# Cross-attention slots: the probabilities' split moved to the head of the slot, the value product into the same slot, the bias a slot behind its load

## The chip, the cores and the metric

One core of one Trainium2 chip runs the whole kernel. The metric is device time in microseconds (us). The kernel before takes 2206.15 us, the median of three runs (2199.84 to 2209.55).

## What is computed

For each of 32 batches there are 512 query rows of 640 channels (`x`) and 77 context rows of 1024 channels (`ctx`), all in float32. There are 20 heads of 32 channels.

```python
q   = heads(x @ to_q_w)
k,v = heads(ctx @ to_k_w), heads(ctx @ to_v_w)
p   = softmax(q @ k.T / sqrt(32))          # 77 keys for each head
out = merge(p @ v) @ to_out_w + to_out_b + x
```

The reference also slices further groups of context rows (object, others, ip) behind row 77. The context has only 77 rows, so these groups are empty and the kernel computes the text branch alone.

Float32 products are made from two parts: a value is split into a high part (a copy rounded to the matmul type) and a low part (value minus high part), and three of the four cross products are summed in PSUM (`PAIRS`). That is why nearly every operand is first copied on ScalarE and then subtracted on VectorE or GpSimd.

## The kernel before, in words

A first phase (lines 210 to 239, up to about 280 us) makes keys, values and split weights from the context and leaves them in DRAM (`k_dram`, `v_dram`, `wo_dram`). Then comes a loop over 160 *slots*: slot n handles batch b = n // 5 and head group j = n % 5 (four heads). All engines get their instructions in the order in which `slot` (lines 522 to 595) writes them; nothing reorders them, so an instruction that waits holds up all that stands behind it on its engine. DMAs are all issued by SyncE (SP), one queue, in the same written order.

For slot n the steps are these. Times of a step are in the profile under the line given.

- `scores(n, t)`, t = 0 to 3 (L335): three matmuls into one of three `sc` banks, then VectorE's maximum (L343). `exps(n, t)` (L353): four exponentials on ScalarE, which write probabilities into one of two buffers `pn` and row sums.
- `normalize(n-1)` (L364, L365): VectorE's reciprocal of the sums, then GpSimd multiplies the previous slot's probabilities in place.
- `transpose_p(n-1)` (L372, L379): VectorE transposes them into the single buffer `z`; four DMAs write `z` to the DRAM scratch `pd`.
- `load_p(m)` (L388, L389): two DMAs read `pd` of an older slot m back, with keys on the partitions, into the single buffer `raw`.
- `cast_p(m)` (L396, ScalarE, 128x1024) and `rest_p(m)` (L402 VectorE, L405 ScalarE 64x512, L406 GpSimd): split `raw` into `pp`, two buffers. This is "the split of probabilities". In the steady state it is done three slots after the scores, m = n-3 (`SPLIT_LAG`), between the second and third scores of slot n.
- `values(m)` (L420): eight matmuls of `pp` with the values `vb` into the one bank `pa`, then `split_a` into `at`. It is done four slots after the scores, m = n-4 (`TAKE_LAG`).
- `queries(n+1)` (L317): fifteen matmuls into the single bank `pq`, then `split_q` (L100 ScalarE, L101 VectorE) into one of two `qt`, which `scores(n+1, ...)` need.
- `piece(b', i)` (L449): the output projection of an older batch, in ten pieces of twelve matmuls, two pieces in each slot. `finish` (L477, L481): VectorE adds a finished bank to the residual row block `xr`, and SP writes it out. `load_residual` and `add_bias` (L438, L442) load `xr` (two buffers) and add the bias on GpSimd, both in the same slot.
- `load_x` (L256), `transpose_x` (L261), `split_x` (L268, L269): the next batch's `x`, single buffer `xs`, is loaded at the start of a slot with j = 4, transposed in j = 0 and 1, and split in j = 2 (two of five) and j = 3 (three of five). `queries` needs it in the slot j = 4.
- `refill` (L294, L304): keys of heads j = 0, 1 are reloaded in j = 2, those of j = 2, 3, 4 in j = 1; values of j = 0, 1 in j = 3 and those of j = 2, 3, 4 in the next batch's j = 0. A values load is seven DMAs in pieces of 77, 48, 29, 77, 16, 61 and 61 rows, and each row is cut into runs of 256 bytes.

The first four slots run beside the end of the context phase. Buffers `raw`, `pp`, `at`, `xr` and the weights `wo_s` exist only from slot 4 on (`LATE`). After slot 159, `end` (lines 597 to 643) splits and multiplies what is still under way, makes the last pieces of batch 30 and the whole projection of batch 31; its residual blocks are loaded one by one in the last loop (line 639).

Of the kernel before, what the change touches and what calls it, by code (L numbers as in the profile page):

```python
# [50 lines left out]
def kernel(  # L51
# [207 lines left out]
    def transpose_x(b, i):  # L259
        part = xss[b][:, 4 * i : 4 * i + 4, :].rearrange("p a u -> p (a u)")  # L260
        nc.vector.transpose(part, part)  # L261
# [67 lines left out]
    def scores(n, t):  # L329
        b, j = divmod(n, NC_)  # L330
        g = GROUP_OF[j]
        qt, kb = qts[n % 2], kbs[g][:, j - GROUPS[g][0]]
        sc = ps.tile([P, S], F32, tag="sc", name="sc", bufs=3)
        for m, (a, c) in enumerate(PAIRS):
            nc.tensor.matmul(  # L335
                sc[:, :KCOLS],
                qt[:, a, t * P : (t + 1) * P],
                kb[:, c, :],
                start=(m == 0),
                stop=(m == 2),  # L340
            )
        nm = main.tile([P, HPC], F32, tag="nm", name="nm", bufs=2)
        nc.vector.tensor_reduce(  # L343
            nm, sc[:, :KCOLS].rearrange("p (h k) -> p h k", k=NKEY), AX.X, ALU.max, negate=True
        )
        return sc, nm
# [11 lines left out]
                accum_out=sms[n][:, at : at + 1],  # L358
            )

    def normalize(n):
        pf = pnb[n % 2][:, :, :NKEY]
        rs = main.tile([P, NQ * HPC], F32, tag="rs", name="rs", bufs=2)
        nc.vector.reciprocal(rs, sms.pop(n))  # L364
        nc.gpsimd.tensor_tensor(  # L365
            pf, pf, rs.unsqueeze(2).to_broadcast([P, NQ * HPC, NKEY]), ALU.mult
        )
# [16 lines left out]

    def load_p(n):
        pd = pds.pop(n)
        raw = late[0].tile([P, 3, S], F32, tag="raw", name="raw", bufs=1)
        nc.sync.dma_start(raw[:, 0:2, :], pd[0 : 2 * P, :].rearrange("(k p) q -> p k q", p=P))  # L388
        nc.sync.dma_start(raw[:64, 2, :], pd[2 * P :, :])  # L389
        raws[n] = raw  # L390

    def cast_p(n):

        raw = raws[n]
        pp = late[0].tile([P, 5, S], FPR, tag="pp", name="pp", bufs=2)
        nc.scalar.copy(pp[:, 0:2, :], raw[:, 0:2, :])  # L396
        pps[n] = pp

    def rest_p(n):

        raw, pp = raws.pop(n), pps[n]
        nc.vector.tensor_tensor(  # L402
            pp[:, 2:4, :], raw[:, 0:2, :], pp[:, 0:2, :].bitcast(F32), ALU.subtract
        )
        nc.scalar.copy(pp[:64, 4, :], raw[:64, 2, :])  # L405
        nc.gpsimd.tensor_tensor(  # L406
            pp[64:, 4, :], raw[:64, 2, :], pp[:64, 4, :].bitcast(F32), ALU.subtract
        )
# [24 lines left out]
        split(at[:, 0, :], at[:, 1, :], pas.pop(n))  # L433
        ats[n] = at

    def load_residual(b, t):
        xr = late[0].tile([P, C], F32, tag="xr", name="xr", bufs=2)
        nc.sync.dma_start(xr, x[b, t * P : (t + 1) * P, :])  # L438
        xrs[b, t] = xr

    def add_bias(b, t):
        nc.gpsimd.tensor_tensor(xrs[b, t], xrs[b, t], bias, ALU.add)  # L442
# [37 lines left out]
            if h == 1:  # L480
                nc.sync.dma_start(out[b, t * P : (t + 1) * P, :], xr)  # L481

    def residual(b, t):
        load_residual(b, t)
        add_bias(b, t)

    LATE = 4
    SPLIT_LAG, TAKE_LAG = 3, 4

    splits = {LATE: [0], LATE + 1: [1, 2], LATE + 2: [3]}  # L490
    takes = {LATE + 1: [0], LATE + 2: [1, 2], LATE + 3: [3]}
    for n in range(4, N):
        splits[n + SPLIT_LAG] = [n]
        takes[n + TAKE_LAG] = [n]


    PIECES = {3: (1, 0), 4: (1, 2), 0: (2, 4), 1: (2, 6), 2: (2, 8)}
    RESIDUAL = {3: (1, 0), 4: (1, 1), 0: (2, 2), 1: (2, 3)}
    TRANSPOSE_X = {0: (0, 1), 1: (2, 3)}
    SPLIT_X = {2: ((), (0,), (1,)), 3: ((2,), (3,), (4,))}  # L500
    wos = []

    def take(m):
# [2 lines left out]

    def refill(b, j):

        if j == 0 and b >= 2:
            load_values(b - 1, 1)  # L510
        elif j == 1 and b >= 1:
            load_keys(b, 1)
        elif j == 2 and b + 1 < B:
            load_keys(b + 1, 0)
        elif j == 3 and b >= 1:
            load_values(b, 0)
        elif j == 4 and b + 2 < B:
            load_x(b + 2)
        elif j == 4 and b == B - 1:
            load_values(b, 1)  # L520

    def slot(n, beside=None):
        b, j = divmod(n, NC_)
        ahead = n + 1 < N
        back, first = PIECES[j]
        bo_, has_out = b - back, b >= back
        xsplits = SPLIT_X.get(j, ((), (), ())) if b + 1 < B else ((), (), ())
        turns = list(TRANSPOSE_X.get(j, ())) if b + 1 < B else []
        taken, split_now = takes.get(n, []), splits.get(n, [])

        has_residual = j in RESIDUAL and b >= RESIDUAL[j][0]
        upcoming = splits[n + 1][0] if late and splits.get(n + 1, [N])[0] in pds else None

        refill(b, j)
        if n:
            normalize(n - 1)
        s = scores(n, 0)
        finish()
        exps(n, 0, *s)
        if ahead:  # L540
            queries(n + 1, 0, 2)
        s = scores(n, 1)
        if has_residual:
            load_residual(b - RESIDUAL[j][0], RESIDUAL[j][1])
        if n:
            transpose_p(n - 1)
        exps(n, 1, *s)
        for m in split_now[:1]:
            cast_p(m)
        if ahead:  # L550
            queries(n + 1, 2, NC_)
        s = scores(n, 2)
        for m in split_now[:1]:
            rest_p(m)
        for m in split_now[1:]:
            load_p(m)
        if upcoming is not None and len(split_now) < 2:
            load_p(upcoming)
        if has_residual:
            add_bias(b - RESIDUAL[j][0], RESIDUAL[j][1])  # L560
        for c in xsplits[0]:
            split_x(b + 1, c)
        if ahead:
            split_q(n + 1)
        exps(n, 2, *s)
        if has_out:
            piece(bo_, first)
            if j == 2:
                piece(bo_, first + 1)
        finish()  # L570
        for i in turns[:1]:
            transpose_x(b + 1, i)
        for c in xsplits[1]:
            split_x(b + 1, c)
        for m in taken[:1]:
            values(m)
        if beside:
            beside()
        s = scores(n, 3)
        for m in taken[:1]:  # L580
            split_a(m)
        for c in xsplits[2]:
            split_x(b + 1, c)
        exps(n, 3, *s)
        for m in taken[1:]:
            take(m)
        for m in split_now[1:]:
            cast_p(m)
            rest_p(m)
        if upcoming is not None and len(split_now) > 1:  # L590
            load_p(upcoming)
        if has_out and j != 2:
            piece(bo_, first + 1)
        for i in turns[1:]:
            transpose_x(b + 1, i)

    def end():


        last = B - 1  # L600
        normalize(N - 1)
        cast_p(N - 3)
        rest_p(N - 3)
        finish()
        transpose_p(N - 1)
        load_p(N - 2)
        take(N - 4)
        residual(last - 1, 2)
        for i in (4, 5):
            piece(last - 1, i)  # L610
        cast_p(N - 2)
        rest_p(N - 2)
        load_p(N - 1)
        take(N - 3)
        finish()
        residual(last - 1, 3)
        for i in (6, 7):
            piece(last - 1, i)
        take(N - 2)
        finish()  # L620
        for i in (8, 9):
            piece(last - 1, i)
        cast_p(N - 1)
        rest_p(N - 1)
        finish()
        for i, (t, h) in enumerate((t, h) for t in range(NQ) for h in range(2)):
            if i < 3:
                pos[last, t, h] = ps.tile([P, S], F32, tag="sc", name="po", bufs=3)
            elif i == 3:
                pos[last, t, h] = ps.tile([P, S], F32, tag="pq", name="po", bufs=1)  # L630
            elif i < 7:
                output_bank(last, t, h)
            else:
                take(N - 1)
                pos[last, t, h] = late[1].tile([P, S], F32, tag="pa", name="po", bufs=1)
            for j in range(4):
                project(last, t, h, j)
        for t in range(NQ):
            residual(last, t)
            for h in range(2):  # L640
                project(last, t, h, 4)
                closed.append((last, t, h))
            finish()

    with tc.manual_schedule(engines=ENGINES):
# [23 lines left out]
            ctx.enter_context(tc.tile_pool(name="psl", bufs=1, space=PSUM, reuse_waits="tile"))  # L669
        )  # L670
        load_p(0)
        wos.append(late[0].tile([P, NC_, 2, C], FPR, name="wo_s"))
        for n in range(LATE, LATE + 4):
            slot(n)
# [45 lines left out]
```

## Time and profile before

| | |
|---|---|
| median of the three runs | 2206.15 us |
| profiled execution, its own time | 2202.92 us |
| its span | 2201.1 us |
| mean granted TensorE clock | 0.98 |
| TensorE matmul busy / weight load busy | 2042.4 us (93%) / 1802.9 us (82%) |
| ScalarE / VectorE / GpSimd busy | 1381.1 (63%) / 1234.3 (56%) / 1036.1 (47%) |
| DMA: mean share of 16 engines, rate | 72.8%, 188 GB/s |
| first scores of slot 8 on TensorE | 375.3 us |
| end of TensorE's work of slot 159 | about 2123.8 us |

The profile is of one execution, so durations taken from it add up to its own time and not to the median. PE is TensorE's matmul, PEld its weight load, DVE VectorE, ACT ScalarE, POOL GpSimd and SPq SyncE's DMA queue. Matmuls overlap in the pipeline, so a busy PE is not a PE without loss; the wait of the weight loads shows more of it than the wait of the matmuls.

### The profile page before, as it was taken

The numbers are of one execution on the slowest core, as the hardware profiler recorded it, in microseconds if no ns is written. First come the engines' busy times: TensorE is split into PE (matmuls) and PEld (weight loads), VectorE is DVE, ScalarE is ACT, GpSimd is POOL, SyncE is SP. The second block draws the span as 40 slices with busy tenths as digits, with TensorE's granted clock in tenths as the row PEclk, the third lists the DMA queues.
The fourth block names the chain that finished last, engine by engine and source line by source line (L and its number), as shares of the span: only waits on it lengthen the run. The fifth ranks groups of instructions, "written<-read, shape, count | busy, mean of one in ns | idle before, by whom it ended". The sixth has DMA issues, their size and how long they took to land.

```text
span 2201.1 us, 36626 instructions
## 1 busy us (share of the span) xinstructions
PE 2042.4 (93%) x11012; PEld 1802.9 (82%) x11012; DVE 1234.3 (56%) x1996; ACT 1381.1 (63%) x6057; POOL 1036.1 (47%) x618
## 2 busy tenths in 40 slices
PE   9899997999999999999999999999999999999985
PEld 7799975888888888888888888888888888888875
DVE  4433245566665666665566656566556566656651
ACT  3322156677677676777767777776666676777750
POOL 0000134555555555555555555555555555555542
PEclk9999998999999999999999999999999999999998
DMA  8953358877777777777877777787777777778662
GB/s 190 274 164 112 110 120 213 207 204 193 200 201 198 192 196 204 197 185 200 207 200 188 202 195 202 197 205 196 197 200 188 198 198 194 200 198 203 176 172 95
DMA packets 524243, 416.45 MB, mean 189 GB/s; under 512 B 138480, under 2 KB 427760, under 8 KB 524048
## 3 DMA queue, kind: packets, MB, share of 16 engines
q1 hardware_dynamic: 524048, 414.13, 72.8%
q8 instruction: 89, 1.46, 0.3%
q14 instruction: 106, 0.87, 0.1%
HBM read 238.69 MB, written 175.31 MB: 188 GB/s over the span
## 4 chain that ended last, share of the span: by engine, by line
DMA 31%; PE 23%; SPq 12%; issue 10%; POOL 9%; ACT 7%; DVE 6%; POOLq 0%; DVEq 0%; ACTq 0%
DMA raw<-pd 16%; DMA xr<-in_x_dram 7%; PE pk L164 5%; SPq L379 5%; PE pq L317 5%; PE po L449 5%; POOL xt L269 5%; PE pv L190 4%; DMA out_dram<-xr 4%; POOL pn L365 4%; ACT pn L353 3%; PE pa L420 2%; ACT pp L396 2%; PE sc L335 2%; SPq L304 2%
## 5 line engine op out<-in xcount | busy, mean ns | idle before, releaser
L353 ACT ACTIVATE pn<-sc,nm 128x77 f32<-128x77 f32 x2560 | 796.3, 332 | 366.2 <-DVE nm L343 362.6
L317 PE MATMUL pq<-xt,wq_s 128*128 128x512 f32 x2400 | 643.9, 404 | 29.8 <-POOL xt L269 28.2
L449 PE MATMUL po<-wo_s,at 128*128 128x320 f32 x3840 | 609.9, 309 | 9.3 <-DVE xr L477 7.9
L449 PEld LDWEIGHTS po<-wo_s,at 128*128 128x128 f32 x3840 | 573.4, 188 | 12.0 <-DVE xr L477 9.0
L317 PEld LDWEIGHTS pq<-xt,wq_s 128*128 128x128 f32 x2400 | 439.4, 192 | 139.4 <-POOL xt L269 63.2
L353 ACT ACTIVATION_READ_ACCUMULATOR pn<-sc,nm 128x1 f32 x2560 | 539.8, 211 | 0.0
L372 DVE STREAM_TRANSPOSE z<-pn 128x1280 f32<-128x1280 f32 x160 | 241.9, 1512 | 393.9 <-POOL pn L365 392.8
L335 PE MATMUL sc<-kb,qt 128*128 128x308 f32 x1920 | 392.5, 311 | 74.7 <-ACT qt L100 38.6
L335 PEld LDWEIGHTS sc<-kb,qt 128*128 128x128 f32 x1920 | 327.7, 190 | 139.3 <-ACT qt L100 49.1
L406 POOL TENSOR_TENSOR pp<-raw,pp 64x512 fp32r<-64x512 f32 x160 | 266.2, 1664 | 367.8 <-ACT pp L405 365.3
L442 POOL TENSOR_TENSOR xr<-xr,bias 128x640 f32<-128x640 f32 x128 | 201.6, 1575 | 447.4 <-DMA xr<-in_x_dram 374.2
L365 POOL TENSOR_TENSOR pn<-pn,rs 128x1232 f32<-128x1232 f32 x160 | 364.1, 2276 | 49.8 <-DVE rs L364 46.5
L420 PE MATMUL pa<-pp,vb 128*128 128x512 f32 x1280 | 329.1, 400 | 14.4 <-DVE at L101 14.4
L343 DVE TENSOR_REDUCE nm<-sc 128x4 f32<-128x308 f32 x640 | 278.7, 445 | 37.2 <-PE sc L335 36.8
L420 PEld LDWEIGHTS pa<-pp,vb 128*128 128x128 f32 x1280 | 244.8, 197 | 52.9 <-DVE at L101 15.3
L396 ACT CAST pp<-raw 128x1024 fp32r<-128x1024 f32 x160 | 169.1, 1057 | 183.0 <-DMA raw<-pd 181.5
L402 DVE TENSOR_TENSOR pp<-raw,pp 128x1024 fp32r<-128x1024 f32 x160 | 214.4, 1340 | 89.5 <-ACT pp L396 89.5
L269 POOL TENSOR_TENSOR xt<-xs,xt 128x512 fp32r<-128x512 f32 x160 | 201.9, 1284 | 30.5 <-POOL pp L406 12.9
L477 DVE TENSOR_TENSOR xr<-po,xr 128x320 f32<-128x320 f32 x256 | 117.4, 479 | 103.1 <-POOL xr L442 100.4
L164 PE MATMUL pk<-ct,wk_s 128*128 128x512 f32 (+1 forms) x600 | 137.3, 391 | 9.8 <-ACT ct L100 9.8
L190 PE MATMUL pv<-wv_s,ct 128*128 128x320 f32 (+1 forms) x960 | 142.1, 309 | 0.0
L190 PEld LDWEIGHTS pv<-wv_s,ct 128*128 128x128 f32 (+1 forms) x960 | 139.4, 184 | 2.0
(36 smaller groups left out, 1075.1 us busy)
## 6 DMA issues: line engine op xcount, KB each, us to landing
pd<-z SPq DMA_DIRECT2D x640, 160.0 KB
raw<-pd SPq DMA_DIRECT2D x160, 512.0 KB
xs<-in_x_dram SPq DMA_DIRECT2D x128, 320.0 KB
xr<-in_x_dram SPq DMA_DIRECT2D x128, 320.0 KB
out_dram<-xr SPq DMA_DIRECT2D x128, 320.0 KB
raw<-pd SPq DMA_DIRECT2D x160, 128.0 KB
v_dram<-vs SPq DMA_DIRECT2D x19, 640.0 KB
k_dram<-ks SPq DMA_DIRECT2D x20, 512.0 KB
```

The costliest lines, as they stand in the source:

```text
L164: nc.tensor.matmul(pks[j][:, :gn], wk_s[:, k, a, j * P : (j + 1) * P], cts[k][:, c, :gn], start=(k == 0 and n == 0), stop=(k == NK - 1 and ...
L190: nc.tensor.matmul(pv[:tn, :HALF], cts[k][:, a, t0 : t0 + tn], wv_s[:, k, c, h * HALF : (h + 1) * HALF], start=(k == 0 and n == 0), stop=( ...
L269: nc.gpsimd.tensor_tensor(parts[1], src, parts[0].bitcast(F32), ALU.subtract)
L317: nc.tensor.matmul(pqs[n], wq_s[:, k, a, j * P : (j + 1) * P], xts[b, k][:, c, :], start=(k == 0 and m == 0), stop=(k == NC_ - 1 and m == 2),)
L335: nc.tensor.matmul(sc[:, :KCOLS], qt[:, a, t * P : (t + 1) * P], kb[:, c, :], start=(m == 0), stop=(m == 2),)
L343: nc.vector.tensor_reduce(nm, sc[:, :KCOLS].rearrange("p (h k) -> p h k", k=NKEY), AX.X, ALU.max, negate=True)
L353: nc.scalar.activation(pnb[n % 2][:, at, :NKEY], sc[:, i * NKEY : (i + 1) * NKEY], AF.Exp, bias=nm[:, i : i + 1], accum_out=sms[n][:, at : ...
L365: nc.gpsimd.tensor_tensor(pf, pf, rs.unsqueeze(2).to_broadcast([P, NQ * HPC, NKEY]), ALU.mult)
L372: nc.vector.transpose(z.rearrange("p b t j -> p t b j"), pn.rearrange("p (t h) k -> p t (h k)", t=NQ).rearrange("p t (b i) -> p t b i", i=Q),)
L406: nc.gpsimd.tensor_tensor(pp[64:, 4, :], raw[:64, 2, :], pp[:64, 4, :].bitcast(F32), ALU.subtract)
L420: nc.tensor.matmul(pas[n], vb[:, t, :, a], pp[:, c, :], start=(m == 0), stop=(m == len(PASSES) - 1),)
L449: nc.tensor.matmul(pos[b, t, h][:, :HALF], ats[b * NC_ + j][:, a, t * P : (t + 1) * P], wos[0][:, j, c, h * HALF : (h + 1) * HALF], start= ...
```

## The change

The written order of a slot is changed, and with it the number of buffers.

- The split of probabilities stands at the head of the slot: `cast_p(n-3)` is ScalarE's first instruction, and `rest_p(n-3)` follows the first scores. On GpSimd its subtraction now stands ahead of `normalize(n-1)`. Within `rest_p` the small ScalarE copy comes ahead of VectorE's subtraction.
- `values(n-3)` stands in the same slot, so the lag from scores to values falls from four slots to three.
- `pp` has one buffer instead of two, `raw` two instead of one, `xr` three instead of two, `nm` three instead of two.
- `load_p(n-2)` stands ahead of `transpose_p(n-1)` and its four writes, not behind them.
- `transpose_p(n-1)` stands behind the third scores and behind `split_q`, not ahead of the second exponentials.
- `add_bias` takes a block that was loaded in the slot before.
- `load_x` stands in the second half of the slot j = 4, not at its start; `transpose_x` is spread over j = 0 and 1, `split_x` over j = 1 (one), 2 (two) and 3 (two).
- Keys of j = 2, 3, 4 are reloaded in j = 0, values of j = 0, 1 in j = 1, and values of j = 2, 3, 4 in j = 3 of the same batch.
- The pieces of the projection begin one slot earlier (slot 7, j = 2 of the next batch), two in every slot; four pieces instead of six are left for `end`.
- `end` has one value product less to do, loads the last batch's residual blocks early (one into a `raw` buffer) and adds all four biases ahead of the last projection.

```diff
-        pp = late[0].tile([P, 5, S], FPR, tag="pp", name="pp", bufs=2)
+        pp = late[0].tile([P, 5, S], FPR, tag="pp", name="pp", bufs=1)
...
-        raw = late[0].tile([P, 3, S], F32, tag="raw", name="raw", bufs=1)
+        raw = late[0].tile([P, 3, S], F32, tag="raw", name="raw", bufs=2)
...
-        xr = late[0].tile([P, C], F32, tag="xr", name="xr", bufs=2)
+            xr = late[0].tile([P, C], F32, tag="xr", name="xr", bufs=3)
...
-    PIECES = {3: (1, 0), 4: (1, 2), 0: (2, 4), 1: (2, 6), 2: (2, 8)}
-    RESIDUAL = {3: (1, 0), 4: (1, 1), 0: (2, 2), 1: (2, 3)}
-    TRANSPOSE_X = {0: (0, 1), 1: (2, 3)}
-    SPLIT_X = {2: ((), (0,), (1,)), 3: ((2,), (3,), (4,))}
+    PIECES = {2: (1, 0), 3: (1, 2), 4: (1, 4), 0: (2, 6), 1: (2, 8)}
+    RESIDUAL = {1: (1, 0), 2: (1, 1), 3: (1, 2), 4: (1, 3)}
+    BIAS = {2: (1, 0), 3: (1, 1), 4: (1, 2), 0: (2, 3)}
+    TRANSPOSE_X = {0: ((), (0,), (1,)), 1: ((2,), (3,), ())}
+    SPLIT_X = {1: ((), (0,)), 2: ((1,), (2,)), 3: ((3,), (4,))}
...
-        if j == 0 and b >= 2:
-            load_values(b - 1, 1)
+        if j == 0 and b >= 1:
+            load_keys(b, 1)
         elif j == 1 and b >= 1:
-            load_keys(b, 1)
+            load_values(b, 0)
         elif j == 2 and b + 1 < B:
             load_keys(b + 1, 0)
         elif j == 3 and b >= 1:
-            load_values(b, 0)
-        elif j == 4 and b + 2 < B:
-            load_x(b + 2)
```

The body of the slot after the change, in its written order:

```python
        refill(b, j)
        if taken is not None:
            cast_p(taken)
        if n:
            rs = sums(n - 1)
        s = scores(n, 0)
        if taken is not None:
            rest_p(taken)
        if n:
            normalize(n - 1, rs)
        exps(n, 0, *s)
        ...
        s = scores(n, 1)
        finish()
        ...
            load_residual(b - RESIDUAL[j][0], RESIDUAL[j][1])
        if n - LAG + 1 in pds and n > LATE:
            load_p(n - LAG + 1)
        ...
            add_bias(b - BIAS[j][0], BIAS[j][1])
        exps(n, 1, *s)
        ...
        s = scores(n, 2)
        if ahead:
            split_q(n + 1)
        exps(n, 2, *s)
        if n:
            transpose_p(n - 1)
        ...
            piece(bo_, first)
        ...
        finish()
        if j == 4 and b + 2 < B:
            load_x(b + 2)
        if taken is not None:
            values(taken)
        ...
        s = scores(n, 3)
        if taken is not None:
            split_a(taken)
        ...
        exps(n, 3, *s)
        if has_out:
            piece(bo_, first + 1)
```

## The prediction

> **What bounds the kernel now.** I read the page's first part, then the matmul and weight-load waits from slot 8 on, then TensorE's order of time, SP's order of time and DMA rates by stage. The page calls PE 93% busy, but matmuls overlap. The weight loads' waits (engine, line, releaser: us in all, times, longest) in the stretch from 427 to 2101 us, 29 batches:
>
> ```profile
> PEld pq L317 <- POOL xt L269: 57.0, 77, 2.3
> PEld sc L335 <- ACT qt L100: 40.1, 25, 2.8
> PEld sc L335 <- DVE qt L101: 37.8, 48, 2.2
> ```
>
> With two small rows they sum to 138 us; the matmuls' own waits sum to only 87. TensorE in order of time confirms the larger sum:
>
> ```profile
> 427.67 3.68 PE L449 MATMUL po<-wo_s,at 128*128 128x320 f32 x24
> ...
> 1011.99 1.55 PE L317 MATMUL pq<-xt,wq_s 128*128 128x512 f32 x6
> ...
> 1022.55 1.56 PE L317 MATMUL pq<-xt,wq_s 128*128 128x512 f32 x6
> ...
> 2100.67 3.68 PE L449 MATMUL po<-wo_s,at 128*128 128x320 f32 x24
> 2126.49 0.70 PE L449 MATMUL po<-wo_s,at 128*128 128x320 f32 x3 [2.69 <-DVE xr L477]
> 2140.89 3.78 PE L420 MATMUL pa<-pp,vb 128*128 128x512 f32 x8 [7.36 <-DVE at L101]
> 2172.92 2.03 PE L420 MATMUL pa<-pp,vb 128*128 128x512 f32 x8
> 2176.35 5.55 PE L449 MATMUL po<-wo_s,at 128*128 128x320 f32 x36 [1.40 <-DVE at L101]
> ```
>
> The group x24 comes once a batch: (2100.67 - 427.67) / 29 = 57.69 us a batch. A slot without a wait takes 1022.55 - 1011.99 = 10.56, so 52.8 a batch: **4.9 us of each batch are lost**, 142 in the stretch. The last lines are the tail: PE ends slot 159 at about 2123.8, waits 2.7 and 7.4 us, ends near 2182, and the span ends at 2201.1. The chain of waits says what fills its end:
>
> ```profile
> 2180.31 3.05 DMA xr<-in_x_dram
> 2186.42 2.94 DMA xr<-in_x_dram
> 2192.42 2.95 DMA xr<-in_x_dram
> ```
>
> Three residual blocks are loaded only when the two buffers come free. Why the batch loses 4.9 us is in SP's order of time:
>
> ```profile
> 909.53 1.92 SPq L256 DMA_DIRECT2D xs<-in_x_dram  x4
> ...
> 919.41 6.62 SPq L304 DMA_DIRECT2D vb<-v_dram  x7
> 926.08 2.53 SPq L438 DMA_DIRECT2D xr<-in_x_dram  x1
> 928.71 2.40 SPq L379 DMA_DIRECT2D pd<-z  x4
> 931.22 0.58 SPq L388 DMA_DIRECT2D raw<-pd  x1
> ```
>
> A values load of three heads with the residual load behind it holds SP for 9.1 us (median of 26), one of two heads 6.1. `pd` and `raw` queue behind; the cast then starts at 938.35, ScalarE's `qt` copy stands behind it, and PE waits. The other loss is `split_x`, three fifths of it in the slot before its use.
>
> **What the Trainium skill says.** *Perfetto Trace Analysis*, Identifying the Most-Contended Engine: matmul busy time misleads, since matmuls are pipelined; look at weight loads. The trace agrees (138 against 87). *TensorE: Matmul & The Clock Gate*, What's actually happening: the clock falls to half after an idle window of about 3.4 us. The trace agrees: after 7.36 us idle, eight passes took 3.78, otherwise 2.03. *DMA: Bandwidth & Descriptors*, Why a DMA increments its semaphore by 16 and not by 1: the number of DMA engines used divides the row count, so 61 or 29 rows go to one engine. The stage table agrees: from 926 to 928 us, behind such pieces, the mean share of 16 engines is 0.08 at 18 GB/s, about one sixteenth, while full stages move 270 to 400. So DMA is not short of rate; SP's order is.
>
> **The change, part by part.**
>
> *Start of the late slots.* Before, PE reaches slot 8 at 375.3. Now `cast_p(0)` stands behind slot 4, so that slot no longer waits 4.1 us at its head, but `values(0)` waits for the split instead. Raw lands as before at 334.8; cast, copy and GpSimd end at 337.9 (1.05 + 0.5 + 1.7), the product at 338.4. Slot 5 then takes two products in one `pp`: the second cast waits for the first product (346.5), which costs PE about 4 us; slot 6 ends at about 360.5. Slot 7 already carries two pieces (24 x 0.147 = 3.5) and a product (1.9) more: slot 8 starts at 371, 4 us earlier with 5.4 us more behind it. Uncertain by 5 us either way, with the `wo_s` loads beside.
>
> *Slots 8 to 159.* PE's work is unchanged: 152 x 10.56, less 3.5 for the last slot's missing queries: 1602. What goes: `split_x` now ends on GpSimd early in the slot of its first use, leaving c = 2 to 4 ready a slot ahead (57.0/29 = 2.0 a batch gone); VectorE's `qt` no longer stands behind the transpose that waits for `normalize`; the bias no longer waits for its load (GpSimd's 325 us there were off the path). `xr` loads are no longer held by the output that frees the buffer, except t = 3's; `load_x` no longer stops SP on GpSimd (85.5 us of SP's waits from 700 to 2000). `sums`, `nm` and the moved pieces I cost at nothing: same instructions, beside PE's work; without that cover a reciprocal costs 0.25 a slot.
>
> What is added is a loop. `cast_p` waits for raw, and behind it stand on ScalarE all of the slot's exponentials and `qt`, on VectorE (`rest_p`) two maxima and `qt`, on GpSimd **`normalize`, which before did not wait for raw**. From a cast at c after its slot's start: copy c + 1.55, GpSimd's subtraction + 1.66, normalize + 2.28, transpose + 1.5, four `pd` issues + 2.4: SP is free at c + 9.4. PE's need: the product stands 6.5 us into the slot and its first low pass needs VectorE's part (c + 2.3), so c up to about 4.5 is free.
>
> Two hops of two slots (21.1) carry it round the batch. From j = 2: c2 + 9.4, the three-head values load 9.1, raw's landing 5, less 21.1: c4 = c2 + 2.4. Slot j = 4: `load_x` is issued behind `pd` and an output at c4 + 9.9; its last quarter landed 9.3 us after the first issue before, I take 8.5: it lands c4 + 7.8 into j = 0. SP is limited by DMAs eight back (SP waited for `xs` at L481, 22 times), so `pd` of j = 0 ends about 1.9 later; two-head values and output 6.6, raw 5, less 21.1: c2 of the next batch = c4 + 0.2. Round the batch lateness grows by 2.6; PE must absorb it: **2.5 us lost per batch instead of 4.9**. The disputed size is raw's landing, 3.6 in the empty tail, up to 7.1 behind `pd` and `vb` in the middle: it now stands ahead of `pd`, so I take 5. Two hops make -2.8 to +4.2: from nothing lost to 6.8 a batch, above what is lost now. Other slots (refill 2 us or none) end under c = 4.5. The single `pp` costs nothing there: the product before ends two to four us ahead of the next cast; late casts only move away. The sum of 30.4 batches: 76 us.
>
> *The tail.* PE's work: 48 + 120 projection matmuls (24.7) and three products (5.6), 30.3 against 35.7 before. Waits: GpSimd's part of N-3 about 3.5, raw of N-2 about 3 (its load follows a transpose in slot 159), cold clock and a bank about 1, `split_a` 1.4. All residuals are loaded and biased during the twelve us of projection, so after PE only an add (0.9) and the output (3.1, as before). 42 us against 77.3, the largest certain gain. If raw of N-2 takes 7 us, 45; the bound below is 38.
>
> Sum: 371 + 1602 + 76 + 42 = 2091 of span; the profiled execution had 1.8 around its span and the median lay 3.2 above it: **2096 us**.
>
> **Rivals.**
>
> *PE is the bound.* Raw lands in 3.6 to 4.2, the loop closes: 0 to 1.2 a batch, say 0.4: 371 + 1602 + 12 + 42 + 5 = 2032. For it: full stages move 270 to 400 GB/s. Against: vb alone holds SP 9 us.
>
> *The steady loss stays.* Raw at 6.1, the mean of the landings that ScalarE waited for before: 2.6 + 2.2 = 4.8 a batch: 371 + 1602 + 146 + 42 + 5 = 2166; only both ends gain.
>
> *The loop decides.* Normalize behind raw's split feeds SP's lateness into itself; landings above 7.1 with a fuller queue, and `transpose_x` blocking VectorE for `xs` with maxima behind it, make 8 a batch: 371 + 1602 + 243 + 42 + 5 = 2263, slower. It is slower from (2206 - 2020) / 30.4 = 6.1 a batch on, a landing of 6.8.
>
> That the change doesn't do what it says: the written order on each engine shows it does.
>
> **How the numbers follow.** Forecast (1.2 to 3.6 a batch, 2056 to 2130) 0.48; PE-bound 0.20; loss stays (to 2200) 0.20; loop decides 0.12. From 2020 to 2175 leaves out the loop, the top of "stays" (0.04) and the bottom of "PE-bound" (0.02). About 0.5% is what a measurement of this kernel can tell from no change: faster 0.85, same 0.03 (top of "stays"), slower 0.12.
>
> **What would show it.** Waits on `xt` gone or below 10 us; weight-load waits near 75 us from slot 8, on `pp` and `qt` in j = 4 and on `sc` in j = 1; slots other than j = 1 and 4 at 10.56; casts waiting for raw most in j = 4 and j = 2; span end within 5 us of the last matmul; no `xr` load in the last 10 us. Wrong if PE's slots all run long (DMA or clock), if `xs` stops VectorE in every batch by over 3 us, or if casts come before 2 us into j = 4.

## The result and the profile after

The changed kernel takes 2181.8 us (median of four runs, 2175.3 to 2185.1) against 2204.8 of the kernel before on the same chip: a ratio of 0.9892, interval 0.9857 to 0.9928. It is faster by 1.1%, where 5% were forecast (2096 us); the time lies above the range that was given, 2020 to 2175 us. The profiled execution took 2178.6 us, with a span of 2176.8.

The two spans can be cut at the same places of TensorE's order of time. Slot 159 of the changed kernel now holds a value product and two pieces; it ends half-way through the group of 24 that starts at 2134.06, at about 2135.9.

| part (us) | before | predicted | after |
|---|---|---|---|
| start of slot 8 | 375.3 | 371 | 377.1 |
| slots 8 to 159 | 1748.5 | 1602 + 76 = 1678 | 1758.8 |
| tail | 77.3 | 42 | 40.9 |
| span | 2201.1 | 2091 | 2176.8 |

The tail gained 36.4 as forecast. The slots, which were to gain 70, lost 10. So the question is one place: why a batch still takes 57.8 us.

First the weight loads' waits of the changed kernel in the same stretch as before, 427 to 2101 us (engine, line, releaser: us in all, times, longest):

```profile
PEld sc L335 <- ACT pn L353: 92.2, 28, 5.2
PEld pa L423 <- DVE pp L406: 12.5, 21, 1.1
PEld po L453 <- DVE xr L481: 3.1, 4, 1.4
PEld pa L423 <- ACT pp L399: 1.6, 2, 1.3
```

The waits for `xt` and `qt` are gone, all of them. In their place stands one wait that comes about once a batch: a bank of scores that ScalarE's exponentials have not yet read. TensorE's order of time shows it in the slot j = 1 of two batches that follow each other:

```profile
1000.86 1.14 PE L335 MATMUL sc<-kb,qt 128*128 128x308 f32 x3 [3.11 <-ACT pn L353]
1001.79 3.07 PE L453 MATMUL po<-wo_s,at 128*128 128x320 f32 x12
...
1053.47 2.25 PE L317 MATMUL pq<-xt,wq_s 128*128 128x512 f32 x9
1058.72 0.99 PE L335 MATMUL sc<-kb,qt 128*128 128x308 f32 x3 [3.00 <-ACT pn L353]
1059.51 3.20 PE L453 MATMUL po<-wo_s,at 128*128 128x320 f32 x12
```

From one to the next are 57.9 us. The wait is 3.0; behind it three score matmuls take 0.99 instead of 0.59 and twelve of the projection 3.20 instead of 1.92. Together that is 4.7 of the 5.0 us by which 57.8 exceeds the 52.8 of five undisturbed slots. Why the exponentials are late is on VectorE, in the same slot. Its waits for `x` from 700 to 2000 us, and one of them in order of time:

```profile
DVE xs L261 <- DMA xs<-in_x_dram: 109.4, 23, 5.9
```

```profile
1055.69 0.84 DVE L261 STREAM_TRANSPOSE xs<-xs 128x640 f32<-128x640 f32 x1 [4.64 <-DMA xs<-in_x_dram]
```

Behind this transpose, on the same engine, stands the maximum that the exponentials need. Before the change VectorE did not wait for `x` at all. The load is late because it is issued late; SP's order of time, with ScalarE's cast of the slot j = 4 ahead of it:

```profile
1034.34 1.05 ACT L399 CAST pp<-raw 128x1024 fp32r<-128x1024 f32 x1 [3.60 <-DMA raw<-pd]
```

```profile
1041.71 2.25 SPq L382 DMA_DIRECT2D pd<-z  x4
1044.06 0.69 SPq L485 DMA_DIRECT2D out_dram<-xr  x1
1044.85 2.65 SPq L256 DMA_DIRECT2D xs<-in_x_dram  x4
1047.60 3.16 SPq L294 DMA_DIRECT2D kb<-k_dram  x4
1050.86 0.39 SPq L391 DMA_DIRECT2D raw<-pd  x1
```

The cast at 1034.34 waited for `raw`; its `pd` writes end at 1043.96, 9.6 later, as the prediction worked out; `x` is issued at 1044.85, and is there 10.8 us after that.

The tail, against the lines shown before:

```profile
2125.09 1.91 PE L453 MATMUL po<-wo_s,at 128*128 128x320 f32 x12
2129.12 0.50 PE L423 MATMUL pa<-pp,vb 128*128 128x512 f32 x1 [2.12 <-ACT pp L399]
...
2134.06 3.71 PE L453 MATMUL po<-wo_s,at 128*128 128x320 f32 x24
...
2149.69 14.29 PE L453 MATMUL po<-wo_s,at 128*128 128x320 f32 x96
2163.82 2.03 PE L423 MATMUL pa<-pp,vb 128*128 128x512 f32 x8
2167.25 5.55 PE L453 MATMUL po<-wo_s,at 128*128 128x320 f32 x36 [1.40 <-DVE at L101]
```

The wait of 7.4 is gone, and the span ends 9.6 us after the last group begins, against 24.8 before. The end of the chain of waits holds no load any more, only the matmuls and VectorE's additions:

```profile
2167.25 4.25 PE po L453 x27
2171.50 0.03 DVEq L481
2171.53 1.80 DVE xr L481 x5
```

### The profile page after: what moved, and what is told of

It reads as the page before. It is cut to its first block, busy times and chain, and to the rows that moved or that the text cites. A ratio compares the mean times of both kernels' runs of the same rounds, so it can differ in the third digit from the quotient of the medians.

```text
span 2176.8 us, 37127 instructions
## 1 busy us (share of the span) xinstructions
PE 2043.0 (94%) x11012; PEld 1830.7 (84%) x11012; DVE 1230.4 (57%) x1996; ACT 1377.9 (63%) x6057; POOL 1051.7 (48%) x618
## 4 chain that ended last, share of the span: by engine, by line
PE 37%; DMA 23%; SPq 13%; POOL 10%; ACT 6%; issue 6%; DVE 4%; POOLq 0%; DVEq 0%; ACTq 0%
DMA raw<-pd 11%; PE po L453 10%; DMA xs<-in_x_dram 9%; PE pq L317 8%; PE pk L164 5%; PE pa L423 5%; PE sc L335 5%; POOL pn L368 5%; PE pv L190 5%; POOL pp L409 4%; SPq L304 3%; ACT pn L353 3%; SPq L442 3%; SPq L256 3%; SPq L382 2%
## 5 line engine op out<-in xcount | busy, mean ns | idle before, releaser
L453 PE MATMUL po<-wo_s,at 128*128 128x320 f32 x3840 | 645.3, 319 | 4.4 <-DVE xr L481 2.9
L409 POOL TENSOR_TENSOR pp<-raw,pp 64x512 fp32r<-64x512 f32 x160 | 280.8, 1755 | 701.5 <-ACT pp L405 701.5
L317 PE MATMUL pq<-xt,wq_s 128*128 128x512 f32 x2400 | 611.7, 395 | 2.3 <-ACT xt L268 1.3
L453 PEld LDWEIGHTS po<-wo_s,at 128*128 128x128 f32 x3840 | 604.3, 197 | 6.5 <-DVE xr L481 4.3
L368 POOL TENSOR_TENSOR pn<-pn,rs 128x1232 f32<-128x1232 f32 x160 | 364.2, 2276 | 30.3 <-DVE rs L363 18.1
L423 PE MATMUL pa<-pp,vb 128*128 128x512 f32 x1280 | 345.3, 410 | 24.0 <-ACT pp L399 14.1
L343 DVE TENSOR_REDUCE nm<-sc 128x4 f32<-128x308 f32 x640 | 287.8, 455 | 45.8 <-PE sc L335 45.2
L406 DVE TENSOR_TENSOR pp<-raw,pp 128x1024 fp32r<-128x1024 f32 x160 | 196.0, 1225 | 203.9 <-ACT pp L399 203.9
L101 DVE TENSOR_TENSOR qt<-pq,qt 128x512 fp32r<-128x512 f32 x160 | 110.6, 691 | 148.9 <-ACT qt L100 148.5
L261 DVE STREAM_TRANSPOSE xs<-xs 128x640 f32<-128x640 f32 x128 | 105.5, 826 | 147.1 <-DMA xs<-in_x_dram 140.7
L100 ACT CAST at<-pa 128x512 fp32r<-128x512 f32 x160 | 98.3, 614 | 70.0 <-PE pa L423 69.2
```

The lines of the kernel that those rows point to most:

```text
L317: nc.tensor.matmul(pqs[n], wq_s[:, k, a, j * P : (j + 1) * P], xts[b, k][:, c, :], start=(k == 0 and m == 0), stop=(k == NC_ - 1 and m == 2),)
L343: nc.vector.tensor_reduce(nm, sc[:, :KCOLS].rearrange("p (h k) -> p h k", k=NKEY), AX.X, ALU.max, negate=True)
L368: nc.gpsimd.tensor_tensor(pf, pf, rs.unsqueeze(2).to_broadcast([P, NQ * HPC, NKEY]), ALU.mult)
L409: nc.gpsimd.tensor_tensor(pp[64:, 4, :], raw[:64, 2, :], pp[:64, 4, :].bitcast(F32), ALU.subtract)
L423: nc.tensor.matmul(pas[n], vb[:, t, :, a], pp[:, c, :], start=(m == 0), stop=(m == len(PASSES) - 1),)
L453: nc.tensor.matmul(pos[b, t, h][:, :HALF], ats[b * NC_ + j][:, a, t * P : (t + 1) * P], wos[0][:, j, c, h * HALF : (h + 1) * HALF], start= ...
```

## The experiments

Twelve kernels were run, on several chips, so each is told as a ratio to the kernel before on its own chip. The kernel before itself differs by 0.9% between these chips (2204.6 to 2224.0 us), and the change was timed on one of them only; half a per cent between ratios from two chips is therefore not read as a difference. The theory after the result was this: the loop that the prediction described is closed and sets the period, and `x` is one of its hops. The rivals: `x` stops VectorE by itself, without a loop; or it is a lag of the order on GpSimd alone.

**1. The load of `x` back at the head of j = 4**

```diff
+        elif j == 4 and b + 2 < B:
+            load_x(b + 2)
...
-        if j == 4 and b + 2 < B:
-            load_x(b + 2)
```

> The changed kernel, with the load of the next batch's x back at the head of slot j = 4 (ahead of the residual and raw loads). Theory 'x blocks VectorE' (the maxima of slot j = 0 stand on VectorE behind the transpose that waits 4.6 us for x, the last exponentials come late, and the third scores of j = 1 wait for a bank, 3.1 us and then a cold clock): VectorE's wait for x goes, about 4 us a batch, 2182 - 30 x 4 = 2060 us. Rival 'loop' (SP's lateness through raw, split, normalize, transpose and pd is what costs; the wait for x is only where it shows): the loss moves to the product or qt in j = 4 and j = 0, 2150 us or more. Rival 'DMA rate': the same bytes move in the same time, 2180.

Measured: 0.987 (0.9838 to 0.9902), not to be told from the change itself. VectorE no longer waits for `x`, but the loss reappears at the value product; the weight loads' waits from 427 to 2000:

```profile
PEld pa L423 <- ACT pp L399: 54.5, 37, 3.6
PEld pa L423 <- DVE pp L406: 53.5, 57, 1.1
```

A wait that costs as much as the one removed: "`x` stops VectorE" alone falls.

**2. The transposes of `x` a slot later**

```diff
-    TRANSPOSE_X = {0: ((), (0,), (1,)), 1: ((2,), (3,), ())}
-    SPLIT_X = {1: ((), (0,)), 2: ((1,), (2,)), 3: ((3,), (4,))}
+    TRANSPOSE_X = {1: ((), (0, 1), (2,)), 2: ((3,), (), ())}
+    SPLIT_X = {2: ((0,), (1,)), 3: ((2, 3), (4,))}
```

> The changed kernel, with x loaded where the change put it, but transposed only from the second half of slot j = 1 on, and split in j = 2 and 3. 'x blocks VectorE': the landing is as late as before, about 10.9 us after its issue, but nothing waits for it: 2060 to 2085 us. 'Loop': SP's order and all its delays are the same: 2150 or more, with the loss on other waits. 'DMA rate': 2180.

Measured: 0.9895 (0.986 to 0.993). Here `x` is loaded as late as in the change and VectorE never waits for it, yet nothing is gained. ScalarE's casts show what is late now:

```profile
1042.20 1.05 ACT L399 CAST pp<-raw 128x1024 fp32r<-128x1024 f32 x1
...
1057.45 1.04 ACT L399 CAST pp<-raw 128x1024 fp32r<-128x1024 f32 x1 [5.74 <-DMA raw<-pd]
```

The cast of j = 1 waits 5.7 us for `raw`, which was issued behind the 1.3 MB of `x`; the cast starts 8.3 us after the issue of `raw` at 1049.13. So two roads lead from the load of `x` to the cast of j = 1: over VectorE's transpose, maximum and ScalarE's exponentials, and over `raw`. They arrive at the same time, 24.7 us after the cast of j = 4 in the change and 24.5 here (means). Opening one leaves the other.

**3. The last batch's residuals as before**

```diff
-        load_residual(last, 0)
...
-        load_residual(last, 1)
...
-        for t in (0, 1, 3, 2):
-            add_bias(last, t)
...
         for t in range(NQ):
+            load_residual(last, t)
+            add_bias(last, t)
```

> The changed kernel, with the last batch's four residual blocks loaded and biased one by one in the last loop, as the kernel before does. If the early residuals are what shortened the tail: the last 12 to 16 us come back, 2194 to 2198 us, and the last loop shows three residual loads in the chain. If the tail's gain comes from the order of its products: within 4 us of 2182. With three residual buffers instead of two, one load of the three may be hidden: then 2190.

Measured: 0.9919 (0.9894 to 0.9944). The chain of waits holds the loads again:

```profile
2183.15 2.93 DMA xr<-in_x_dram
...
2189.14 3.12 DMA xr<-in_x_dram
```

From the start of the last group to the end of the span are 25.2 us (2173.10 to 2198.3), against 9.6 in the change: 15.6 us of the tail's 36.4 are this part, by one profile each. The ratios themselves overlap with those of the change, 0.3% being too little to part them.

**4. The kernel before, with only the load of `x` made late**

```diff
-        elif j == 4 and b + 2 < B:
-            load_x(b + 2)
...
         finish()
+        if j == 4 and b + 2 < B:
+            load_x(b + 2)
```

> The kernel before, with only the load of x moved to the second half of slot j = 4, where the change has it. 'x blocks VectorE': VectorE waits for x in j = 0 in this kernel too; the wait of 3 to 5 us falls on the maxima behind it, 2205 + 30 x 3 = 2295 us, at least 2240. 'Loop': the kernel before has no loop through normalize, and the load no longer stops SP on GpSimd's split (85 us of SP's waits): 2205 or faster.

Measured: 1.064 (1.0599 to 1.068). Waits of weight loads and of VectorE, 427 to 2000:

```profile
PEld sc L335 <- ACT qt L100: 142.0, 25, 6.8
```

```profile
DVE xs L261 <- DMA xs<-in_x_dram: 77.8, 19, 5.1
```

The place of the load alone costs 6% in this kernel. Both theories had a part wrong: the loop's said 2205 us or faster, and the other had the loss on VectorE's maxima. TensorE's large wait comes once a batch, 5.7 us on average (142.0 / 25), and ends with ScalarE's half of `qt`. In order of time, that is:

```profile
1128.99 1.04 ACT L396 CAST pp<-raw 128x1024 fp32r<-128x1024 f32 x1 [7.23 <-DMA raw<-pd]
1131.12 1.46 PE L335 MATMUL sc<-kb,qt 128*128 128x308 f32 x3 [6.16 <-ACT qt L100]
```

The `qt` copy stands on ScalarE behind a cast that waits 7.2 us for `raw`, and SP had issued this `raw` behind `x` and behind a values load of three heads that took 9.94 us. VectorE's wait for the same `x` (3.66 us, over 15 us earlier) held up no matmul in this batch. So what the kernel shows is a late `raw` behind `x`, the second of the two roads of kernel 2; that a late `x` on VectorE costs time by itself is not shown by it.

**5. Normalize and transpose ahead of the rest of the split**

```diff
-        if taken is not None:
-            rest_p(taken)
         if n:
             normalize(n - 1, rs)
...
+        if n:
+            transpose_p(n - 1)
+        if taken is not None:
+            rest_p(taken)
...
-        if n:
-            transpose_p(n - 1)
```

> The changed kernel, with normalize and the transpose of the slot before put ahead of rest_p (they no longer stand behind the raw load's split on GpSimd and VectorE); the cast stays at the head, x is loaded where the change has it. Theory 'loop' (raw, split, normalize, transpose, pd, SP, raw goes round in about 57.7 us a batch; the late x is fed by it too, since its load stands behind pd): the loop is cut, pd and x are issued 4 to 7 us earlier in j = 4: 0.945 to 0.965 of the kernel before. Rival 'two walls' (late x alone keeps the batch at 57.7): 0.985 or more, with VectorE's wait for x still 4 us a batch. Rival 'DMA rate': 0.985 or more with no wait for x.

Measured: 0.9395 (0.9377 to 0.9412), a median of 2071.5 us: the fastest version that does all of the work. `x` is still loaded late, and VectorE still waits for it 26 times, but the weight loads wait for one thing only:

```profile
PEld pa L423 <- DVE pp L406: 42.4, 49, 2.5
```

SP's order of time, for a cast of j = 4 at 1043.58:

```profile
1047.94 3.21 SPq L382 DMA_DIRECT2D pd<-z  x4
1051.25 0.44 SPq L485 DMA_DIRECT2D out_dram<-xr  x1
1051.79 2.70 SPq L256 DMA_DIRECT2D xs<-in_x_dram  x4
```

From the cast to the issue of `x` are 8.2 us here, 10.5 in the change. The hop over SP's values load shrinks too, by 1.7.

**6. The same with `x` at the head of j = 4**

```diff
+        elif j == 4 and b + 2 < B:
+            load_x(b + 2)
...
-        if j == 4 and b + 2 < B:
-            load_x(b + 2)
```

> The same, and x loaded at the head of j = 4. 'Loop' and 'two walls' alike: neither is left, 0.93 to 0.95, slots near 10.6 us and the raw load behind values and x the only late one. 'DMA rate': 0.985 or more.

Measured: 0.9576 (0.9556 to 0.9595), slower than the fifth kernel, and a miss. Put early, the 1.3 MB stand ahead of the `raw` that is issued in the slot j = 4; the weight loads' wait on `pp` rises to 76.8 us.

**7. The first kernel without the reload of the values**

Here `x` is at the head of j = 4, as in kernel 1, and from the second batch on the values are not loaded again: later batches use the first batch's.

```diff
-        elif j == 1 and b >= 1:
-            load_values(b, 0)
-        elif j == 3 and b >= 1:
-            load_values(b, 1)
```

> The changed kernel with x loaded at the head of j = 4, and without the values' reload from the second batch on (14 DMAs a batch left out, so later batches are multiplied with the first batch's values). The order on ScalarE, VectorE and GpSimd is as in the change. 'Loop': values hold SP for 9.1 and 6.1 us a batch inside the loop, so it goes round in about 50 us, PE is the bound: 0.93 to 0.945. If split and normalize alone made the loss: 0.97 or more. 'DMA rate' (460 KB of 11.1 MB less): 0.96 or more.

Measured: 0.9308 (0.9293 to 0.9323), against 0.987 with the reload. The order of instructions on ScalarE, VectorE and GpSimd is that of the change, and a batch takes 53.9 us where TensorE's work alone is 52.8. So that order costs about 1 us a batch by itself; the rest of its cost needs the values loads in the round. Whether they cost by SP's time or by their bytes this kernel doesn't part.

**8. The whole split in the middle of the slot, `x` at the head**

```diff
-        if taken is not None:
-            cast_p(taken)
...
-        if taken is not None:
-            rest_p(taken)
...
+        if n:
+            transpose_p(n - 1)
...
         exps(n, 1, *s)
+        if taken is not None:
+            cast_p(taken)
+            rest_p(taken)
...
-        if n:
-            transpose_p(n - 1)
...
```

> The changed kernel with x loaded at the head of j = 4 and the whole split put back to where the kernel before has it (cast after the second exponentials, normalize and transpose ahead of it); values stay in the same slot. 'Loop': it is cut as in the run with the transpose ahead of rest_p, and raw is needed 4 us later in its slot, but the product follows 3 us behind the split: 0.93 to 0.955, within 1% of that run. If the opening cast itself is worth something (ScalarE free early), this is over 1% slower than that run.

Measured: 0.9519 (0.9491 to 0.9548), against 0.9576 with the cast at the head (kernel 6): the cast at the head of the slot is worth nothing by these ratios; 0.6% is lost with it in this setting.

**9 and 10. Each half of kernel 5 alone.** First normalize ahead, transpose left late:

```diff
-        if taken is not None:
-            rest_p(taken)
         if n:
             normalize(n - 1, rs)
+        if taken is not None:
+            rest_p(taken)
```

> The change with one call moved: normalize stands ahead of rest_p in its slot, so that GpSimd normalizes before it needs raw; the transpose of z stays where the change has it, behind the query split. If the loop runs as the prediction put it (a late raw holds GpSimd, GpSimd holds normalize, normalize holds the transpose), this alone cuts it: a ratio to the kernel before of 0.94 to 0.96, as with both moved (0.9395). If the loop also runs through ScalarE and VectorE (the transpose stands behind qt, which stands behind the opening cast and VectorE's part of the split), the release of z moves by some 0.3 us only and the ratio stays at 0.98 or above.

Measured: 0.9845 (0.9803 to 0.9887). Then transpose early, normalize left behind the split:

```diff
+        if n:
+            transpose_p(n - 1)
         if j in BIAS and b >= BIAS[j][0]:
...
         exps(n, 2, *s)
-        if n:
-            transpose_p(n - 1)
```

> The counterpart: the change with the transpose of z moved ahead (behind the load of raw, ahead of the bias), and normalize left behind rest_p. If GpSimd's order makes the loop, nothing is gained: 0.985 to 0.995. If the place of the transpose behind qt makes it, 0.94 to 0.96. If either one alone is worth half and the loop is simply as long as the sum of its pieces, both this and the other kernel lie between, 0.96 to 0.975.

Measured: 1.0092 (1.0063 to 1.0121), which no theory had. The waits of TensorE's loads and of VectorE:

```profile
PEld sc L335 <- DVE qt L101: 76.5, 41, 2.6
```

```profile
DVE z L375 <- POOL pn L368: 381.5, 131, 3.2
```

VectorE now stands at the transpose until GpSimd has normalized, and its part of `qt` stands behind. So neither half is worth much and both together are worth 5%: `z` is held by `raw` over GpSimd (normalize behind the subtraction) and, side by side with that, over ScalarE and VectorE (transpose behind `qt`). In the prediction's working only the first road was in the sum.

**11. Kernel 5 with the values loaded behind `raw`**

```diff
-        elif j == 1 and b >= 1:
-            load_values(b, 0)
-        elif j == 3 and b >= 1:
-            load_values(b, 1)
...
             load_p(n - LAG + 1)
+        if j in (1, 3) and b >= 1:
+            load_values(b, j // 2)
```

> The fastest version so far (normalize and transpose both ahead of rest_p, 0.9395) with the values load of slots 1 and 3 issued behind raw instead of at the slot's head. If the values load ahead of raw is what remains of the loop there (42 us of weight-load waits on pp), 0.925 to 0.935; if its place does not matter, 0.94; if it now makes pd late instead, 0.95 or more.

Measured: 0.996 (0.9937 to 0.9983), the worst of the three cases that were named. `raw` comes early, but the `pd` writes queue behind the values, and `z` has one buffer:

```profile
DVE z L375 <- DMA pd<-z: 140.7, 55, 4.2
```

**12. Half of the bytes of `x`**

```diff
-        xs = main.tile([P, S // Q, C // 4], F32, tag="xs", name="xs")
+        na = S // Q if b < 2 else S // Q // 2
+        if b < 2:
+            xs = main.tile([P, S // Q, C // 4], F32, tag="xs", name="xs")
+        else:
+            xs = xss[b - 1]
         src = x[b].rearrange("(a j) (q u) -> q j a u", j=Q, q=4)
         for q in range(4):
-            nc.sync.dma_start(xs[q * Q : (q + 1) * Q, :, :], src[q])
+            nc.sync.dma_start(xs[q * Q : (q + 1) * Q, 0:na, :], src[q][:, 0:na, :])
```

> The change with half of the x load left out from batch 2 on: each of the four DMAs brings 8 of 16 row groups, the other half of the tile keeps older data; order, instructions and number of DMAs are unchanged. In the trace of the change one round of the batch takes 10.5 from the cast in j = 4 to the issue of x, 10.9 until x can be transposed (or, beside it, 5.8 to the issue of raw and 8.3 until raw is there), 3.0 to the next cast, 10.3 to the one of j = 2, 17.9 to raw's issue and 4.6 to the cast of j = 4: 57.8, which is the period. If these 1.28 MB ahead of both x's transpose and raw are the term that my sum had too small (8.5 for 10.9), half of them brings both waits in some 2 to 3 us earlier, the round to about 55, and the time to a ratio of 0.945 to 0.96, near the predicted 2096 over 2206 = 0.950. If another round of the same length stands behind (as when only VectorE's wait for x was taken away), the ratio stays at 0.98 or above.

Measured: 0.9424 (0.9383 to 0.9466). Order, instructions and number of DMAs are those of the change, and the time falls to just below the forecast's ratio of 2096 / 2206 = 0.950. VectorE's wait for `x` from 427 to 2000 us shrinks from 123.1 to a sixth (its lines stand four further down here):

```profile
DVE xs L265 <- DMA xs<-in_x_dram: 20.1, 25, 1.3
```

Both roads of kernel 2 open at once here, and the gain is there. This shows that the landing of `x` is a hop of the round; with kernels 1 and 2 it shows that it has to be shortened for both who wait for it. A rival is that fewer bytes speed up every transfer: in the table below the other hops of kernel 12, the landing of `raw` for j = 4 among them, are as long as in the change or longer, so it is not that. (The hops listed in the expectation add up to 57.2, not 57.8; the table has the means.)

## Why the prediction was wrong: the round, hop by hop

The prediction had the loop, its places (j = 2, j = 4, j = 1) and its sum. The round can be measured in each kernel from the order of time of SP, ScalarE and VectorE: means over the 20 to 23 batches from 690 to 1990 us. One round is one batch.

| hop (us) | predicted | change | 2 transposes late | 9 normalize first | 10 transpose early | 5 both | 12 half `x` |
|---|---|---|---|---|---|---|---|
| cast of j = 4 to issue of `x` | 9.9 | 10.55 | 10.54 | 9.92 | 10.56 | 8.42 | 10.53 |
| issue of `x` to its first transpose | 8.5 | **10.97** | (21.19) | 10.82 | 10.90 | 10.74 | 7.16 |
| from there to the cast of j = 2 | 13.5 | 13.58 | (3.83) | 14.07 | 15.10 | 13.67 | 14.37 |
| that cast to issue of `raw` for j = 4 | 18.5 | 17.93 | 18.09 | 18.73 | 18.17 | 16.20 | 18.06 |
| landing of this `raw`, to the cast | 5.0 | 4.87 | 4.83 | 4.78 | 5.43 | 5.33 | 4.93 |
| round | 55.4 | 57.9 | 58.5 | 58.3 | 60.2 | 54.4 | 55.0 |
| (round - 57.9) x 30.2 | | 0 | +18 | +12 | +69 | -107 | -86 |
| span less the change's 2176.8 | | 0 | +11.7 | +10.8 | +68.2 | -104.0 | -85.6 |

In brackets: the second kernel transposes after the cast of j = 1, so its road is over `raw`, and only the sum of the two cells counts. The factor is the 151 slots from slot 8 to slot 159, in batches. The last two lines agree within 7 us, but this only checks the measuring: five stretches that lead from a cast to the same cast a batch later add up to the period in any kernel, whatever sets it. That the round sets it must show in waits at the hops' ends. In the change the cast of j = 4 waits for `raw` in 21 of 21 batches (3.5 us on average), and the first transpose waits for `x` in 21 of 21 (4.7). In kernel 12 the cast still waits every time (3.8) and the first transpose only 0.9 us on average. In kernel 5 the cast of j = 4 waits in 15 of 22 batches, 0.6 us on average, and in kernel 10 in 3 of 21: there this round no longer sets the pace alone.

- *Start.* 377.1, predicted 371, uncertain by 5. Raw and the first product were right (338.23, predicted 338.4; the second wait 4.4, predicted 4). What was missing is the clock after these waits: the products behind them took longer. The lines of TensorE's order of time:

```profile
338.23 0.79 PE L423 MATMUL pa<-pp,vb 128*128 128x512 f32 x1 [5.82 <-ACT pp L399]
339.49 3.08 PE L423 MATMUL pa<-pp,vb 128*128 128x512 f32 x7 [0.47 <-DVE pp L406]
...
354.04 0.80 PE L423 MATMUL pa<-pp,vb 128*128 128x512 f32 x1 [4.40 <-ACT pp L399]
355.29 3.35 PE L423 MATMUL pa<-pp,vb 128*128 128x512 f32 x7 [0.46 <-DVE pp L406]
...
377.13 0.59 PE L335 MATMUL sc<-kb,qt 128*128 128x308 f32 x3
```

 Eight matmuls of a product take 3.9 and 4.2 us here, 2.0 otherwise: 4 of the 6 us. The granted clock is 0.50 from 336 to 342 us.
- *What goes.* The waits for `xt` and `qt`, the bias wait (GpSimd's 325 us, now 1), SP's stop at `load_x`: right. `sums`, `nm` and the moved pieces at nothing: right; no wait of TensorE names them.
- *The landing of `raw`.* The prediction called it the disputed size and took 5; it is 4.87 where it counts. The range was spread on the wrong term.
- *The landing of `x`: the step that failed.* "Its last quarter landed 9.3 us after the first issue before, I take 8.5." It is 10.97 (10.3 to 12.1). That is 2.5 us of each round, and the whole difference between the predicted 55.4 and the measured 57.9; the other hops miss by -0.6 to +0.7 and cancel. The prediction went below the number that it had, and gave it no bounds. It also carried that number to another place in the queue. Before, SP had issued nothing for 4.0 us (3.6 to 4.7) when `x` went out; the load ahead of the `x` at 909.53 was this:

```profile
904.93 0.65 SPq L389 DMA_DIRECT2D raw<-pd  x1
```

 In the change `x` goes out 0.1 us behind four `pd` writes and an output. Further transfers follow within 10 us in both. The head of the slot by itself doesn't make the difference: in kernel 1 `x` is back there, but again right behind `pd` and an output, and SP's last wait for `x` ends 11.0 us after the first issue (mean of 23). No kernel varies what stands ahead of `x` alone, so this reason for the longer landing is not shown; that the length of this hop mattered is shown by kernel 12.
- *From `x` to the cast of j = 2.* The number was right (13.5 for 13.58) by luck, for the road was not: it was taken over SP (`pd`, the two-head values, `raw`), and it is over VectorE's transpose and ScalarE's exponentials, or over the `raw` of j = 0. The prediction named the sign of its own failure, "if `xs` stops VectorE in every batch by over 3 us"; the mean wait is 109.4 / 23 = 4.8.
- *Where it shows on TensorE.* Expected on `pp` and `qt` in j = 4 and on `sc` in j = 1, near 75 us; it is on `sc` in j = 1 nearly alone, 92 of 109 us, and the lower clock behind each adds 1.7 a batch. *TensorE: Matmul & The Clock Gate* of the Trainium skill, What's actually happening, cited in the prediction, gives an idle window of about 3.4 us; here 3.0 was enough in the batch shown, where the granted clock is 0.50 from 1059 to 1062 us.
- *The tail.* 40.9 for 42, and the two pieces of it for their reasons: right. The terms listed (30.3 + 3.5 + 3 + 1 + 1.4 + 0.9 + 3.1) add up to 43.2, so 42 was 1.2 short of its own terms. Kernel 3 shows the share of the residuals.

Of the rivals, "the steady loss stays" gave 2166 and ends nearest, but its reason (`raw` at 6.1) is not what happened. The mechanism is that of "the loop decides", at 5.2 us a batch instead of 8: below the 6.1 from which it would have been slower. The new round happens to be as long as the old loss, which it replaced; that is why a large change moved the time by 1%. "PE is the bound" is refuted for the change, and TensorE isn't at its bound in kernel 5 either (54.4 against 52.8).

Is the DMA the limit? On average it is not: the mean share of the 16 DMA engines is 0.76 from 427 to 2000 us in the change, 0.78 in kernel 5. The average hides the hop that was mis-sized. These are two stretches of the round shown above, from the issue of `x` to its first transpose, and from the cast of j = 2 to the issue of `raw` (busy us and number of instructions of PE, PEld, DVE, ACT and POOL, then granted clock, share of the 16 engines, GB/s):

```profile
1044.85:1055.69 10.84, 10.84 (x61) 9.51 (x59) 4.14 (x5) 5.11 (x27) 5.57 (x3) 1.00 1.10 209
1069.63:1087.38 17.75, 17.75 (x102) 16.18 (x101) 11.59 (x19) 16.04 (x70) 13.97 (x10) 1.00 0.60 157
```

While `x` lands the DMA engines are full, in every one of 17 batches (1.08 to 1.13; the share adds up the time that packets took, so it can pass 1). In the other stretch they are not, and SP is busy in this way:

```profile
1079.57 5.16 SPq L304 DMA_DIRECT2D vb<-v_dram  x7
1084.77 2.51 SPq L442 DMA_DIRECT2D xr<-in_x_dram  x1
```

*Perfetto Trace Analysis* of the Trainium skill, Optimizing DMA Performance, distinguishes a kernel bound on the engines from one bound on the sequencer that issues. This trace has a stretch of each kind: the hop of `x`, with full engines and shorter by 3.8 us with half of the bytes, fits the first, and the hop of 17.9 us in part the second, since SP spends 7.9 us of it (mean) on the values and the residual behind them. Kernel 7, which leaves out the values in this hop and in j = 1, shows what they are worth (0.987 to 0.9308). So the prediction's "DMA is not short of rate; SP's order is" holds for the values and fails for `x`, the term that it mis-sized.

Open: why the full engines move only 209 GB/s while `x` lands, when the prediction found stages of 270 to 400, and why 1.3 MB take 10.97 us where half take 7.16. Taking the keys or `raw` from behind `x`, or `pd` and the output from ahead of it, was not tried. That kernel 11 loses by `z`'s single buffer is argued from its waits; a second `z` was not tried.

## What to carry to other kernels

When a change turns an order into a loop over several engines and queues, write the round as a sum of hops, look for a second road beside every hop, check that each hop ends in a wait, and compare the sum with the work of the engine you want to be the bound: the longest round is the period. Give every landing that the change moves to another place in a queue its own bounds, and don't take it shorter than it was measured. Read the DMA share in the hop itself, not as a mean over the kernel. If taking one wait away gains nothing, look at who else waits for the same transfer before you call that transfer harmless; shorten the transfer instead of hiding one of its readers.

## What the runs showed of the hardware

- A load of 1.3 MB in runs of 640 bytes, issued right behind four writes of `pd` and an output and with other loads behind it, is usable 10.97 us after its first issue (mean of 21), with the 16 DMA engines at a share of 1.1; half of it in the same place 7.16 (mean of 23).
- `raw`, half as many bytes as `x`, is cast 4.9 us after its issue where the cast waits for it in j = 4, and 8.0 where it stands behind the load of `x` (kernel 2, mean of 22).
- A TensorE wait of 3.0 us is followed by a granted clock of 0.50 for 3.4 us: twelve passes in 3.20 us for 1.92.
